# Recording the statistics of layer 1's norm at other places among the evacuations of a q and k set

## The chip, the cores and the metric

The kernel runs on one core of one Trainium2 chip. The metric is device time in microseconds (us) of a whole execution; lower is better. Engines: PE is TensorE (matmuls), PEld its weight load, DVE is VectorE, ACT is ScalarE, POOL is GpSimd, SP issues most DMAs.

## The reference

Two layers of masked attention over 64 graphs of 256 nodes with 512 features. Each normalises, applies Relu, attends within the graph and adds to x.

```python
h = jnp.maximum(_layernorm(x), 0.0)
x = x + _L0_gnn_ref(h, adj, Wq, Wk, Wv, Wo, bo)       # 4 heads of 64
h = jnp.maximum(_layernorm(x), 0.0)
x = x + _L1_gnn_ref(h, adj, gamma, beta, w_qkv, w_out, b_out)   # 8 heads of 64
```

`_L1_gnn_ref` begins with a second norm, of h itself:

```python
mu = jnp.mean(x, axis=-1, keepdims=True)
var = jnp.mean(jnp.square(x - mu), axis=-1, keepdims=True)
h = (x - mu) * jax.lax.rsqrt(var + LN_EPS) * gamma + beta
```

So layer 1 needs statistics twice for each row: those of x, and those of Relu(x - mean).

## The kernel before

A step is two graphs (512 rows: NT = 4 tiles of 128 rows, 512 features each), and there are NSTEP = 32 steps. The function `fast_path` doesn't loop over steps: it makes a list of events, each with a due time (period times 6.4 plus a place within the period), sorts it, and calls the functions in that order (L1251). The four compute engines run their instructions in the order in which these calls record them, so a place is a position in each engine's queue. Work of three steps is interleaved: while step s - 1 is in layer 1, layer 0 of step s is finished and its layer 1 norm begins, and layer 0 of step s + 1 is started.

**Projections.** A product of matrices is split Strassen-like into 7 products, numbered 1 to 7 and issued in the order SET = (1, 6, 5, 2, 7, 3, 4). `project_qk` (L791) issues 8 matmuls of 256 columns for each (L803), and returns a function that evacuates the bank. `at_set` spreads a set over one unit of places: product i is due at place + i/7, its evacuation at place + (i+1)/7 - 0.001 (`at_dense`, L1059). The set of this study is layer 1's second q and k set, recorded at AT_QK = 3.5 (L1209), so that its evacuations are due at 3.642 (product 1, on ACT, L737), 3.785 (6, DVE, L739), 3.928 (5, DVE, L741), 4.070 (2, ACT, L745), 4.213 (7, DVE, L743), 4.356 (3, DVE, L747) and 4.499 (4, DVE, L749).

**Banks.** Four banks serve all such products. Three are used twice: the second product is added onto the first in the bank, once that has been read out.

```python
SHARED = {2: 1, 4: 7, 3: 5}
```

**Layer 1's norm.** `norm1(s, k)` (L625) takes row tile NORM1[k] of the step's x: bn_stats and bn_aggr on DVE (`moments`, L574 to L577), then on ACT a negation of the mean (L633) and Relu(x - mean) into h (L634). x comes from layer 0's output (`combine` at AT_C0 = 3.0), whose last additions are POOL's (L771). `norm1_rest(s, k)` (L640) does `moments` of h, and with the fourth tile POOL makes row scales of all (L649, L650, and L586 to L588, `row_scales`). At 4.4998 ACT scales the rows (`scale_row`, L592), then DVE turns blocks of them (L686) and SP moves them.

**What else is recorded near.** At 4.499 ACT places the rows of the following step's layer 0 (`place_h`, L709), at 4.4995 POOL makes the sums of it that products need (`act_sums0`, `act_sums1`, L409 to L414); from 4.4997 the visit of the attention pair of heads: key sums on PE (L1007), reciprocals on DVE (L1029), weighted values (L976) and their copies on ACT (L988), scores (L920), masks on DVE (L944), exponentials on ACT (L949). From 4.5 PE runs layer 0's q and k set of the following step (L803 again), where POOL's sums are read from the second product on.

For the first and the last step (edge 0 and 1) there are other places; steps 1 to 30 (edge 2) take the third tuple of each row of the diff.

Of the kernel before, what the change touches and what calls it, by code (L numbers as in the profile page):

```python
# [315 lines left out]
def fast_path(  # L316
# [739 lines left out]
    def at(period, place, fn, *args):  # L1056
        events.append((period * (PERIOD if period >= 0 else FIRST) + place, len(events), fn, args))
# [52 lines left out]
    p = NSTEP - 2  # L1110
# [15 lines left out]
    for s in range(NSTEP):  # L1126

        p = s - 2
# [40 lines left out]
        p = s - 1  # L1169
        if s == 0:  # L1170
            p -= 2.23 / FIRST
        edge = 0 if s == 0 else 1 if s == NSTEP - 1 else 2
# [11 lines left out]
            else:  # L1184
                at_dense(p, AT_C0 + i / 14, 1 / 14, combine, s, 0, n)
        for k in range(NT):
            at(p, ((2.901, 3.041, 3.181, 3.321), (2.99919, 2.99933, 2.99947, 2.99961), (3.7, 3.72, 3.8, 3.82))[edge][k], norm1, s, k)
            at(
                p, ((3.042, 3.182, 3.322, 3.323), (2.99948, 3.2, 3.3, 3.45), (3.95, 4.02, 4.09, 4.2))[edge][k],
                norm1_rest, s, k,  # L1190
            )
            at(p, (10.9 + 0.1 * k, 6.5 + 0.1 * k, 5.6 + 0.01 * k)[edge], second_bias, s, k)
            place = ((3.6112, 3.6113, 3.7502, 3.7503)[k], 3.6 + 0.01 * k, AT_Q0 - 0.0002 + 0.00001 * k)[edge]
            at(p, place, scale_row, s, NORM1[k])
            if edge == 2:
                at(p, AT_Q0 + (0.15, 0.16, 0.29, 0.3)[k], turn_blocks, s, 1, NORM1[k])
# [8 lines left out]
        p = s  # L1205
        if s < NSTEP - 1:
# [3 lines left out]
            p, place = (s + 1, 1.0) if s < NSTEP - 2 else (s, LAST_QK + 2)  # L1210
# [4 lines left out]
        else:  # L1215
            p = s - 1
# [38 lines left out]
def kernel(tc, *args):  # L1255
    nc = tc.nc
    B, N, _ = args[0].shape
    P = 128
    with tc.tile_pool(name="guard", bufs=1) as guard:
        extremes = guard.tile([P, B // 2 * 6], FP, name="extremes")  # L1260
        ident = guard.tile([P, P], FP, name="ident")
        make_identity(nc, ident)
        fast_path(tc, *args, ident, extremes)
        safe = guard.tile([1, 1], I32, name="safe")
        with tc.tile_pool(name="gps", bufs=1, space=bass.MemoryType.PSUM) as ps:
            top = guard.tile([P, 1], FP, name="top")
            nc.vector.tensor_reduce(top, extremes, axis=mybir.AxisListType.X, op=ALU.max)
            row = ps.tile([1, P], FP, name="row")
            nc.tensor.transpose(row, top, ident)
            all_top = guard.tile([1, 1], FP, name="all_top")  # L1270
            nc.vector.tensor_reduce(all_top, row, axis=mybir.AxisListType.X, op=ALU.max)
            nc.vector.tensor_scalar(safe, all_top, LIMIT, None, op0=ALU.is_le)
        flag = nc.values_load(safe[0:1, 0:1], min_val=0, max_val=1, skip_runtime_bounds_check_because="a comparison gives 0 or 1")
        with tc.If(flag < 1):
            general_path(tc, *args)
# [29 lines left out]
```

## Time and profile before

| | |
|---|---|
| median of 3 runs | 3263.24 us (3262.0 to 3267.05) |
| profiled execution | 3261.14 us, its span 3259.3 us |
| TensorE clock granted | 0.999 |
| DMA | 237.04 MB, mean 73 GB/s |

The span is what the trace covers. In the lines of a timeline the first number is the start in us from the span's start, the second the duration in us (of all when several are merged), then engine, source line, operation, output and input tiles, and how many; a bracket gives the idle time before and what ended it. In a line of waits the numbers are total us, times, and the longest.

### The profile page before, as it was taken

How to read it: one execution, taken by the hardware profiler on the slowest of the kernel's cores; microseconds unless marked ns; L12 is line 12 of the kernel's file. 1: busy time of each engine (PE TensorE's matmuls, PEld its weight loads, DVE VectorE, ACT ScalarE, POOL GpSimd, SP SyncE). 2: the span in 40 equal slices, each digit the busy share in tenths (PEclk: the TensorE clock that was granted, in tenths of full speed). 3: DMA queues.
4: the chain of work that ended last, by engine and by line, in shares of the span. 5: the costliest groups of instructions: out<-in, count | busy, mean ns of one | idle time of the engine just before them, and what ended most of it. 6: DMA issues, size and time to landing. Idle time of an engine off the chain costs nothing.

```text
span 3259.3 us, 59763 instructions
## 1 busy us (share of the span) xinstructions
PE 3204.8 (98%) x22002; PEld 2611.8 (80%) x22002; DVE 2095.1 (64%) x3680; ACT 1256.6 (39%) x2226; POOL 2241.4 (69%) x2124
## 2 busy tenths in 40 slices
PE   9999999999999999999999999999999999999999
PEld 6787878888887888788787888888787888878777
DVE  6656666666666666676666666666666666666665
ACT  4434343343433334343434334343333434343431
POOL 7776776777766767667677677776776766767653
PEclk9999999999999999999999999999999999999999
DMA  4122232232322322223223222222232222322211
GB/s 147 43 85 77 55 85 65 79 82 53 85 69 73 88 60 71 76 67 86 76 55 85 62 82 81 53 84 66 75 86 62 72 70 73 86 72 57 85 31 47
DMA packets 214217, 237.04 MB, mean 73 GB/s; under 512 B 75032, under 2 KB 128416, under 8 KB 213920
## 3 DMA queue, kind: packets, MB, share of 16 engines
q1 hardware_dynamic: 213488, 232.76, 26.0%
q8 instruction: 177, 2.90, 0.4%
q14 instruction: 120, 0.98, 0.1%
q10 hardware_dynamic: 432, 0.40, 0.0%
HBM read 86.12 MB, written 33.62 MB: 37 GB/s over the span
## 4 chain that ended last, share of the span: by engine, by line
PE 66%; POOL 13%; DVE 11%; DMA 5%; SPq 4%; issue 1%; ACT 0%; POOLq 0%; DVEq 0%; ACTq 0%
PE mm L803 26%; PE mm L860 12%; PE sc L976 9%; PE mm L830 7%; PE sc L920 6%; DVE bs L576 5%; SPq L1041 4%; PE mm L1007 3%; POOL xt L498 3%; DMA xt<-in_x_dram 2%; POOL xt L771 2%; POOL n L563 2%; PE mm L920 2%; DVE p L944 2%; DMA oT<-oT 2%
## 5 line engine op out<-in xcount | busy, mean ns | idle before, releaser
L803 PE MATMUL mm<-hT,wqkv 128*128 128x256 f32 x3584 | 795.7, 381 | 31.7 <-DVE qk L743 31.7
L803 PEld LDWEIGHTS mm<-hT,wqkv 128*128 128x128 f32 x3584 | 675.7, 190 | 144.8 <-DVE qk L743 43.7
L953 POOL TENSOR_TENSOR pd<-p 128x512 f32<-128x512 f32 x383 | 479.7, 1274 | 328.1 <-ACT p L949 327.6
L860 PE MATMUL mm<-wo,oT 128*128 128x256 f32 x2632 | 588.3, 381 | 7.6 <-POOL oT L412 5.2
L860 PEld LDWEIGHTS mm<-wo,oT 128*128 128x128 f32 x2632 | 498.9, 191 | 87.1 <-issue 8.8
L1029 DVE RECIPROCAL oT<-mm 128x128 f32<-128x128 f32 x376 | 345.6, 940 | 249.6 <-PE mm L1007 245.6
L949 ACT ACTIVATE p<-p 128x512 f32<-128x512 f32 x766 | 439.6, 626 | 137.0 <-DVE p L944 137.0
L944 DVE TENSOR_TENSOR p<-sc,n 128x512 f32<-128x512 f32 x579 | 363.5, 684 | 113.9 <-PE sc L920 112.5
L844 PE MATMUL mm<-wqkv,hT 128*128 128x256 f32 x1792 | 401.9, 382 | 0.0
L803 PE MATMUL mm<-hT,wqk 128*128 128x256 f32 x1792 | 398.9, 382 | 0.3 <-ACT qk L737 0.2
L803 PEld LDWEIGHTS mm<-hT,wqk 128*128 128x128 f32 x1792 | 338.2, 191 | 56.3 <-issue 10.7
L844 PEld LDWEIGHTS mm<-wqkv,hT 128*128 128x128 f32 x1792 | 335.5, 190 | 53.8 <-issue 10.7
L976 PE MATMUL sc<-p,v 128*32 128x256 f32 x6128 | 350.0, 379 | 1.0 <-issue 1.0
L976 PEld LDWEIGHTS sc<-p,v 128*32 128x32 f32 x6128 | 199.7, 110 | 132.9 <-issue 1.8
L988 ACT COPY oT<-sc 128x512 f32<-128x512 f32 x188 | 109.4, 582 | 500.2 <-PE sc L976 495.3
L1046 POOL TENSOR_TENSOR oT<-oT 128x512 f32<-128x512 f32 x188 | 240.0, 1277 | 83.2 <-DMA oT<-oT 73.5
L920 PE MATMUL sc<-qk 64*128 64x256 f32 x2320 | 292.6, 385 | 0.0
L920 PEld LDWEIGHTS sc<-qk 64*128 64x128 f32 x2320 | 218.7, 186 | 58.8 <-issue 39.6
L771 POOL TENSOR_TENSOR xt<-xt,u 128x512 f32<-128x512 f32 x183 | 228.9, 1272 | 4.4 <-DVE xt L760 1.9
L830 PE MATMUL mm<-wv,hT 128*128 128x256 f32 x1024 | 227.0, 379 | 0.4 <-DVE qk L747 0.4
L830 PEld LDWEIGHTS mm<-wv,hT 128*128 128x128 f32 x1024 | 194.2, 190 | 27.3 <-DVE qk L747 0.7
L592 ACT ACTIVATE h<-h,mr,r 128x512 f32<-128x512 f32 x252 | 184.6, 804 | 0.0
(139 smaller groups left out, 3781.8 us busy)
## 6 DMA issues: line engine op xcount, KB each, us to landing
h<-blocks SPq DMA_DIRECT2D x960, 64.0 KB, 2.0
oT<-oT SPq DMA_DIRECT2D x1504, 32.0 KB, 1.9
xt<-in_x_dram SPq DMA_DIRECT2D x31, 1024.0 KB, 5.8
h<-in_x_dram SPq DMA_DIRECT2D x31, 1024.0 KB, 5.5
out_dram<-xt SPq DMA_DIRECT2D x31, 1024.0 KB, 4.5
ne<-row SPq DMA_DIRECT2D x30, 256.0 KB, 4.7
ad<-in_adj_dram SPq DMA_DIRECT2D x32, 128.0 KB, 8.7
wr<-in_L_gnn_w_qkv_dram SPq DMA_DIRECT2D x3, 1024.0 KB, 9.2
```

The lines of the kernel that those rows point to most:

```text
L771: (nc.vector if last else nc.gpsimd).tensor_tensor(r, r, u, ALU.add)
L803: nc.tensor.matmul(bank[:, k, :], w[:, wa, c, k, a * P:(a + 1) * P], st["hT"][:, ba, c, :], start=first and (k, c) == (0, 0), stop=(k, c) ...
L830: nc.tensor.matmul(bank, st["hT"][:, b0 + t // NIC * step, c % HC, i:i + P], wv0[:, c, :], start=(c == 0), stop=(c == NC - 1),)
L844: nc.tensor.matmul(bank[:, t, :], st["hT"][:, ba, c, t * P:(t + 1) * P], wqkv1[:, wa, c, 2, :], start=first and (t, c) == (0, 0), stop=(t, ...
L860: nc.tensor.matmul(bank[:, t, :], oT[:, ba, c, t * P:(t + 1) * P], w[:, wa, c, :], start=first and (t, c) == (0, 0), stop=(t, c) == (NIC - ...
L920: nc.tensor.matmul(sc[g][e][:, kc, :], qk[rows, 1, k0:k0 + P], qk[rows, 0, g * N:(g + 1) * N], start=True, stop=True,)
L944: nc.vector.tensor_tensor(p[e][:, g], sc[e], neg[:, :, g, :], ALU.add)
L949: nc.scalar.activation(p[e][:, g], p[e][:, g], AF.Exp, scale=SCALE)
L953: nc.gpsimd.tensor_tensor(pd[:, e], p[e][:, :, 0, :], p[e][:, :, 1, :], ALU.add)
L976: nc.tensor.matmul(po[r0:r0 + 32, g, :], st[f"v{lyr}"][:, g * NIC + kc, pr * P + r0:pr * P + r0 + 32], p[r0 // DH][:, g, kc, :], start=(kc ...
L1029: nc.vector.reciprocal(inv[:, k * P:(k + 1) * P], sums[:, k * P:(k + 1) * P])
L1046: nc.gpsimd.tensor_tensor(dst, dst, invb, ALU.mult)
```

## The change

Only two lines of the event list differ, and in them only the tuple for steps 1 to 30: the places of `norm1` and `norm1_rest`. No instruction is added or removed.

```diff
         for k in range(NT):
-            at(p, ((2.901, 3.041, 3.181, 3.321), (2.99919, 2.99933, 2.99947, 2.99961), (3.7, 3.72, 3.8, 3.82))[edge][k], norm1, s, k)
+            at(p, ((2.901, 3.041, 3.181, 3.321), (2.99919, 2.99933, 2.99947, 2.99961), (3.79, 3.8, 3.94, 3.95))[edge][k], norm1, s, k)
             at(
-                p, ((3.042, 3.182, 3.322, 3.323), (2.99948, 3.2, 3.3, 3.45), (3.95, 4.02, 4.09, 4.2))[edge][k],
+                p, ((3.042, 3.182, 3.322, 3.323), (2.99948, 3.2, 3.3, 3.45), (4.08, 4.22, 4.23, 4.37))[edge][k],
                 norm1_rest, s, k,
             )
```

Against the evacuations of the set, the order before is: evacuation 1; norm1 k0, k1; evacuation 6; norm1 k2, k3; evacuation 5; norm1_rest k0, k1; evacuation 2; norm1_rest k2, k3; evacuations 7, 3, 4. After: evacuations 1, 6; norm1 k0, k1; evacuation 5; norm1 k2, k3; evacuation 2; norm1_rest k0; evacuation 7; norm1_rest k1, k2; evacuation 3; norm1_rest k3; evacuation 4.

## The prediction

> **What bounds the kernel now.** I read the busy shares first, then the waits of the tensor engine (PE), then the timeline of one visit to the place that the diff names, on each engine. The times 1541 to 1603 us are one period of some 100 us; the 30 steady periods (layer 1's norm of steps 1 to 30) look alike.
>
> ```profile
> PE 3204.8 (98%) x22002; PEld 2611.8 (80%) x22002; DVE 2095.1 (64%) x3680; ACT 1256.6 (39%) x2226; POOL 2241.4 (69%) x2124
> ```
>
> PE is the bound; no other engine is above 69%. So time can be won only where PE pauses or takes longer than it must. The waits of PE (total us, times, longest) say where it pauses:
>
> ```profile
> PE mm L803 <- DVE qk L743: 31.7, 30, 1.8
> PE mm L720 <- ACT h L618: 6.9, 2, 6.7
> PE mm L860 <- POOL oT L412: 5.2, 1, 5.2
> ```
>
> Only the first comes every period, once in each. L803 is the matmul of a q and k set, L743 the evacuation of its product 7. Product 4 goes into the bank that product 7 has left (the table SHARED), so it can't start before VectorE (DVE) has read product 7 out. The PE timeline of the visit, and of the set that follows (layer 0's, as many matmuls of the same size), start and duration first:
>
> ```profile
> 1541.07 10.52 PE L803 MATMUL mm<-hT,wqkv 128*128 128x256 f32 x48
> 1552.45 1.99 PE L803 MATMUL mm<-hT,wqkv 128*128 128x256 f32 x8 [0.86 <-DVE qk L743]
> 1554.38 1.07 PE L1007 MATMUL mm<-pd,ones 128*32 128x256 f32 x16
> ...
> 1562.49 12.35 PE L803 MATMUL mm<-hT,wqk 128*128 128x256 f32 x56
> 1574.68 7.07 PE L830 MATMUL mm<-wv,hT 128*128 128x256 f32 x32
> ```
>
> From first matmul to the first of the next stage the undisturbed set takes 1574.68 - 1562.49 = 12.19 us, the stalled one 1554.38 - 1541.07 = 13.31. The loss is 1.12 us here, more than the 0.86 named, because a matmul's modelled end covers part of the gap. Read in the same way, the first q and k set of layer 1 takes 12.19 (1589.79 to 1601.98). Over the 30 visits the stalled set takes 13.01 to 14.54 us, mean 13.51. So the whole loss is (13.51 - 12.19) x 30 = 39.6 us, 1.2% of the time. Why the evacuation is late, DVE shows:
>
> ```profile
> 1545.76 0.67 DVE L739 TENSOR_TENSOR qk<-mm,qk 128x512 f32<-128x512 f32 x1
> ...
> 1547.96 0.66 DVE L741 TENSOR_TENSOR qk<-mm,qk 128x512 f32<-128x512 f32 x1
> 1548.54 0.69 DVE L576 BATCH_NORM_STATS2 bs<-h 128x6 f32<-128x512 f32 x1
> ...
> 1549.36 0.66 DVE L576 BATCH_NORM_STATS2 bs<-h 128x6 f32<-128x512 f32 x1
> ...
> 1550.15 0.66 DVE L576 BATCH_NORM_STATS2 bs<-h 128x6 f32<-128x512 f32 x1
> ...
> 1550.95 0.66 DVE L576 BATCH_NORM_STATS2 bs<-h 128x6 f32<-128x512 f32 x1
> ...
> 1551.74 0.66 DVE L743 TENSOR_TENSOR qk<-mm,qk 128x512 f32<-128x512 f32 x1
> 1552.32 0.68 DVE L747 TENSOR_TENSOR qk<-mm,qk 128x512 f32<-128x512 f32 x1
> ```
>
> Product 7's evacuation stands behind all four second statistics, recorded ahead of it. Before these, DVE had waited 2.18 us for GpSimd (POOL) to finish xt (L771), then done four first statistics. The queue never empties between.
>
> **What the Trainium skill says.** "Perfetto Trace Analysis", Identifying the Most-Contended Engine: busy matmul time is no good measure of the room left; the trace agrees (98% busy, 1.12 us lost where 0.86 is shown). The same page, Tensor Engine Instruction: ACT, DVE and GpSimd are strict FIFO; the DVE lines agree, L743 starting 0.79 us after the last bn_stats though its bank was ready long before. "PSUM — Partial Sum Buffer", PSUM bank collisions raise a hardware error: the hardware does not arbitrate two engines on one bank, so product 4's wait is needed and only an earlier evacuation shortens it; 30 waits in 30 periods agree. "SBUF — State Buffer", Who interferes with whom: a DVE instruction with one SBUF input, outside two-port modes, doesn't contend with GpSimd; bn_stats reads one, and L771 stays within 1256 to 1290 ns, so I charge nothing for new overlap.
>
> **The change, part by part.** I count t from the set's first matmul (1541.07). A product is 8 matmuls at 12.09/56 = 0.216 us (the chain gives the layer 0 stage of 56 matmuls at L860 as 12.09), so 1.73 us. Its evacuation can start 2.04 after its first matmul (1554.49 for L749, less 1552.45). Products 6, 5, 2, 7, 3, 4 are thus ready at t = 3.77, 5.49, 7.22, 8.94, 10.67, 12.4. A statistics pair (bn_stats, bn_aggr) holds DVE 0.82 after an evacuation, 0.79 after another pair (1548.54, 1549.36, 1550.15); an evacuation 0.58.
>
> - *First statistics (norm1).* k = 0, 1 move from 3.70, 3.72 to behind product 6's evacuation (due 3.785), k = 2, 3 from before to behind product 5's (3.928). Nothing is removed or added: 8 pairs, 6.4 us of DVE a period in both kernels. DVE now: evacuation 6 at 3.77, k0 4.36, k1 5.18, evacuation 5 at 5.97, k2 6.55, k3 7.37. xt is ready from POOL at 2.77 to 3.57 in 29 visits, 4.30 in the first: so k0 no longer waits for POOL.
> - *Second statistics (norm1_rest).* All four stood before evacuation 7 (due 4.213). Now k0 alone does (4.08), k1 and k2 follow it, k3 follows evacuation 3. So k0 8.16, evacuation 7 at 8.95, its data ready at 8.94. PE takes 0.71 from that start to product 4 (1551.74 to 1552.45): 9.66, and product 4 is due at 6 x 1.73 = 10.36. The wait vanishes with 0.70 us to spare. In the layer 1 set at 1589.79, evacuation 7 starts at 8.93 and no wait shows. Then k1 9.53, k2 10.35, evacuation 3 at 11.14, k3 11.72, evacuation 4 at 12.54, over by 13.2; the reciprocals (L1029) are due at 12.19 + 1.14 = 13.33. Gain: all of 39.6 us, if what follows is in time.
> - *ACT.* norm1 also issues a negation and a Relu (0.2 and 0.72 us) on ACT. k0's Relu ends at 6.5, k3's at 9.4, each ahead of its second statistics (8.16, 11.72). Product 2's evacuation, recorded behind k3's Relu, moves from 7.99 to about 9.5. Its bank and rows wait for the scores at 1558.83, t = 16.4 after the gain: hidden by 6 us.
> - *POOL.* The row scales (L649, L650, L586 to L588) end 2.87 us after the last bn_stats starts (1550.95 to 1553.82): 14.6 instead of 12.75. Behind them are the sums over layer 0's hT:
>
> ```profile
> 1553.62 0.20 POOL L588 TENSOR_TENSOR mr<-mr,r 128x4 f32<-128x4 f32 x1
> 1555.71 1.28 POOL L409 TENSOR_TENSOR hT<-hT 128x512 f32<-128x512 f32 x1 [1.90 <-ACT hT L709]
> 1557.08 1.28 POOL L412 TENSOR_TENSOR hT<-hT 128x512 f32<-128x512 f32 x1
> ```
>
> They could start at 14.64 - 1.32 = 13.3 and start at 14.7; L412's, wanted first, ends at 17.4, and PE reads it in the second product of layer 0's set at 12.19 + 8.11 + 1.73 = 22.0. Cover 4.6 us.
> - *Scaled rows.* ACT applies them (L592) behind the output copies, at 17.05 after the gain: 2.4 us after 14.6. The moved steps issue no DMA and pass nothing on SP.
>
> Sum: 3261.14 (profiled execution: span 3259.3 and 1.84 around it) - 39.6 = 3221.5. The median shown lies 2.10 higher, 3263.24: **3223.6**, given as 3223.5.
>
> **Rivals.**
> 1. *Part of the wait stays (about 3243).* Evacuation 7 has 0.70 us of slack behind seven DVE slots. A delay of 1.4 us in that queue would leave half the loss, 20 us. For: the POOL chain before xt varies by 0.8 us between visits. Against: xt is needed only at 4.36, and a late xt pushes fewer statistics in front of evacuation 7 (five pairs for eight), so it can't be later than before.
> 2. *The loss moves down (3263).* PE starts the next stage 1.3 us earlier and then waits for a chain that isn't PE's. For: POOL and DVE carry chains through DMA. Against: PE waits nowhere else every period, and these chains start from PE's own sums and scores, so they move up with it.
> 3. *Slower (about 3286).* ACT is one queue: if the row scales come after 17.05, L592 holds it, behind it the exponentials and the evacuation of layer 0's product 1. This ends at 1565.15 and PE needs its bank at 1562.49 + 3 x 1.73 = 1567.7. So PE loses time once the scales are 2.4 + 2.5 = 4.9 us later than counted, and more than was gained from 6.2; at 7 us it is 0.8 x 30 = 23 us slower. Only the move of k3 works towards this, and it makes 1.9.
> 4. *The order isn't what the numbers say.* Due times sort by value; all eight places fall between the evacuations named. I give it no chance of its own.
>
> **How the numbers follow.** Full gain 0.76 (3218 to 3229: between 42 and 34 us gained, with the spread of 3262 to 3267 in mind); rival 1 0.12; rival 2 0.06; rival 3 0.06. The measurement tells about 0.2%, 6.5 us, from no change: faster 0.88, same 0.06, slower 0.06. The range reaches into rival 1: 3217 to 3243.
>
> **What would show it.** Right: PE's wait on L743 at L803 gone or below 3 us in all; the set at 12.2 us to the key sums; DVE's wait on L771 gone; evacuation 7 near t = 9.0; POOL's wait for L709's hT gone. Wrong: a new periodic line in PE's waits (L803 on ACT L737, or on POOL L409 to L414), or L743 still there, behind k0.

## The result and the profile after

The changed kernel takes 3223.9 us (median, 3222.97 to 3224.88), against 3264.55 us for the kernel before measured beside it. The ratio is 0.9876, 95% interval 0.9858 to 0.9893: 1.2% faster, 40.7 us by the medians. The profiled execution took 3224.29 us, its span is 3222.4 us.

Busy shares of the kernel after, from the page. The span is 36.9 us shorter; PE's idle time fell by 28.7 of these (from 54.5 to 25.8), its busy time by 8.2. So about a fifth of what the stall cost had been shown as busy time.

```profile
PE 3196.6 (99%) x22002; PEld 2613.9 (81%) x22002; DVE 2091.9 (65%) x3680; ACT 1256.4 (39%) x2226; POOL 2240.0 (70%) x2124
```

The waits of PE in the kernel after (total us, times, longest). The wait of L803 on L743 fell from 31.7 us in 30 to 0.6 us in one, at 26.35 us in the program's first q and k set, which the change doesn't reach; none is left in the 30 visits, and no other line of this list comes once a period.

```profile
PE mm L720 <- ACT h L618: 7.6, 3, 6.6
PE mm L860 <- POOL oT L412: 5.8, 2, 5.5
PE mm L860 <- DVE xt L760: 3.1, 6, 0.7
PE mm L803 <- DVE qk L743: 0.6, 1, 0.6
```

PE's timeline of one visit of the kernel after (start, duration). The set is one run of 56 matmuls and the key sums follow 1536.25 - 1524.07 = 12.18 us after its start. Over the 30 visits the mean is 12.18, against 13.51 before; (13.51 - 12.18) x 30 = 39.9 us, close to the 40.7 us by the medians.

```profile
1524.07 12.25 PE L803 MATMUL mm<-hT,wqkv 128*128 128x256 f32 x56
1536.25 1.07 PE L1007 MATMUL mm<-pd,ones 128*32 128x256 f32 x16
```

DVE's timeline of the same visit. Evacuation 6 (L739) now comes when PE has made it ready, no longer behind the wait for POOL; one second statistic (bs<-h) stands ahead of evacuation 7 (L743), and this starts at t = 8.92, 1.75 us earlier than at 1551.74 before (t = 10.67).

```profile
1527.79 0.69 DVE L739 TENSOR_TENSOR qk<-mm,qk 128x512 f32<-128x512 f32 x1 [2.83 <-PE mm L803]
...
1530.01 0.66 DVE L741 TENSOR_TENSOR qk<-mm,qk 128x512 f32<-128x512 f32 x1
...
1532.20 0.66 DVE L576 BATCH_NORM_STATS2 bs<-h 128x6 f32<-128x512 f32 x1
...
1532.99 0.66 DVE L743 TENSOR_TENSOR qk<-mm,qk 128x512 f32<-128x512 f32 x1
1533.57 0.68 DVE L576 BATCH_NORM_STATS2 bs<-h 128x6 f32<-128x512 f32 x1
...
1536.57 0.66 DVE L749 TENSOR_TENSOR qk<-mm,qk 128x512 f32<-128x512 f32 x1
1537.39 1.77 DVE L1029 RECIPROCAL oT<-mm 128x128 f32<-128x128 f32 x2 [0.16 <-PE mm L1007]
```

POOL in the same visit: the row scales (L588 is their last) now end where the sums over layer 0's hT could already have begun; the 1.90 us wait in front of L409 is gone.

```profile
1538.44 0.20 POOL L588 TENSOR_TENSOR mr<-mr,r 128x4 f32<-128x4 f32 x1
1538.60 1.28 POOL L409 TENSOR_TENSOR hT<-hT 128x512 f32<-128x512 f32 x1
1539.96 1.27 POOL L412 TENSOR_TENSOR hT<-hT 128x512 f32<-128x512 f32 x1
```

### The profile page after: what moved, and what is told of

It reads as the page before. It is cut to its first block, busy times and chain, and to the rows that moved or that the text cites. A ratio compares the mean times of both kernels' runs of the same rounds, so it can differ in the third digit from the quotient of the medians.

```text
span 3222.4 us, 59733 instructions
## 1 busy us (share of the span) xinstructions
PE 3196.6 (99%) x22002; PEld 2613.9 (81%) x22002; DVE 2091.9 (65%) x3680; ACT 1256.4 (39%) x2226; POOL 2240.0 (70%) x2124
## 4 chain that ended last, share of the span: by engine, by line
PE 93%; DMA 2%; POOL 2%; SPq 1%; issue 1%; DVE 1%; POOLq 0%; DVEq 0%
PE mm L803 36%; PE mm L860 17%; PE mm L844 10%; PE sc L976 10%; PE sc L920 8%; PE mm L830 7%; PE mm L1007 3%; PE mm L920 2%; SPq L1041 1%; DMA xt<-in_x_dram 1%; POOL xt L498 1%; PE mm L886 0%; DMA h<-in_x_dram 0%; DVE oT L1029 0%; PE mm L549 0%
## 5 line engine op out<-in xcount | busy, mean ns | idle before, releaser
L803 PE MATMUL mm<-hT,wqkv 128*128 128x256 f32 x3584 | 787.5, 380 | 0.0
L803 PEld LDWEIGHTS mm<-hT,wqkv 128*128 128x128 f32 x3584 | 678.2, 190 | 102.4 <-issue 11.4
L860 PE MATMUL mm<-wo,oT 128*128 128x256 f32 x2632 | 587.9, 381 | 9.1 <-POOL oT L412 5.8
L860 PEld LDWEIGHTS mm<-wo,oT 128*128 128x128 f32 x2632 | 498.2, 190 | 89.0 <-issue 7.7
L803 PE MATMUL mm<-hT,wqk 128*128 128x256 f32 x1792 | 398.9, 382 | 0.8 <-DVE qk L743 0.6
L803 PEld LDWEIGHTS mm<-hT,wqk 128*128 128x128 f32 x1792 | 338.2, 191 | 56.8 <-issue 11.2
L920 PEld LDWEIGHTS sc<-qk 64*128 64x128 f32 x2320 | 218.9, 186 | 58.9 <-issue 39.6
L592 ACT ACTIVATE h<-h,mr,r 128x512 f32<-128x512 f32 x252 | 184.6, 804 | 0.0
```

What stands on the lines that cost most here:

```text
L803: nc.tensor.matmul(bank[:, k, :], w[:, wa, c, k, a * P:(a + 1) * P], st["hT"][:, ba, c, :], start=first and (k, c) == (0, 0), stop=(k, c) ...
L860: nc.tensor.matmul(bank[:, t, :], oT[:, ba, c, t * P:(t + 1) * P], w[:, wa, c, :], start=first and (t, c) == (0, 0), stop=(t, c) == (NIC - ...
L920: nc.tensor.matmul(sc[g][e][:, kc, :], qk[rows, 1, k0:k0 + P], qk[rows, 0, g * N:(g + 1) * N], start=True, stop=True,)
```

## Experiments: which part of the change makes the gain

The theory: the gain is what lies between product 5's and product 7's evacuation in DVE's queue. Rivals: it is the filling of DVE's 2.2 us wait for POOL, or the spreading as such, or the amount of DVE's work in the set. Each run is stated as a difference from the changed kernel or from the kernel before, and none leaves out work of the reference. As in the prediction, t counts from the set's first matmul. Diffs of norm1_rest's places show only the end of the line, the tuple for steps 1 to 30.

**First half only.** From the changed kernel:

```diff
-(4.08, 4.22, 4.23, 4.37))[edge][k],   # norm1_rest
+(3.96, 4.02, 4.09, 4.2))[edge][k],
```

> The changed kernel with only its first half: norm1 at its new places, norm1_rest back at the old ones (3.96 for k0, so that it stays behind norm1 k3). Ahead of evacuation 7 stand four second statistics, behind norm1 k2 and k3. Theory (what counts is how many statistics stand between product 5's and product 7's evacuation on VectorE): evacuation 7 starts at t = 5.94 + 0.58 + 6 x 0.80 = 11.3, the set takes 14.0 us, 1.8 more than in the changed kernel, so 3224 + 54 = 3278 us, slower than the kernel before. Rival (the gain is the filling of VectorE's 2.2 us wait for GpSimd ahead of the first statistics): VectorE no longer waits, so 3224 to 3235.

3275.6 us, ratio to the kernel before 1.0043 (1.0029 to 1.0057): slower than it. Its PE waits:

```profile
PE mm L803 <- DVE qk L743: 46.1, 31, 1.7
```

DVE's timeline of a visit at 2960.2: evacuation 6 is as early as in the changed kernel and DVE doesn't wait for POOL, yet evacuation 7 starts at t = 11.31, behind six statistics (two first ones, k2 and k3, and all four second ones).

```profile
2963.92 0.69 DVE L739 TENSOR_TENSOR qk<-mm,qk 128x512 f32<-128x512 f32 x1 [2.83 <-PE mm L803]
...
2966.14 0.66 DVE L741 TENSOR_TENSOR qk<-mm,qk 128x512 f32<-128x512 f32 x1
...
2970.71 0.66 DVE L576 BATCH_NORM_STATS2 bs<-h 128x6 f32<-128x512 f32 x1
...
2971.51 0.66 DVE L743 TENSOR_TENSOR qk<-mm,qk 128x512 f32<-128x512 f32 x1
```

So filling DVE's wait is worth nothing here, and that rival falls.

**Second half only.** The kernel before with the new places of norm1_rest:

```diff
-(3.95, 4.02, 4.09, 4.2))[edge][k],
+(4.08, 4.22, 4.23, 4.37))[edge][k],
```

> The kernel before with only the second half of the change: norm1 at its old places, norm1_rest at the new ones. Theory: VectorE still waits for GpSimd ahead of the first statistics, but only one second statistic stands ahead of evacuation 7, at t = 2.8 to 3.6 + 4.6, so at most 8.2, before its bank is ready at 8.94: the whole gain, 3224 us. Rival (filling the wait): nothing is filled, 3260 us or more.

3222.3 us, 0.9882 (0.9866 to 0.9897): the whole gain, with norm1 untouched. The set takes 12.18 us.

**Two moves only.** The kernel before, k2 and k3 of norm1_rest put right behind evacuation 7:

```diff
-(3.95, 4.02, 4.09, 4.2))[edge][k],
+(3.95, 4.02, 4.22, 4.23))[edge][k],
```

> The kernel before with only norm1_rest k2 and k3 moved, to just behind evacuation 7 (4.22, 4.23). Theory: evacuation 7 starts 6.0 us after the first statistic, which GpSimd lets start at t = 2.8 to 3.6, so at 8.9 to 9.6, within the 9.65: the whole gain from two moves, 3224 to 3226 us. Rival (the first statistics have to move too, or the second ones have to be spread): 3240 or more.

3223.3 us, 0.9882 (0.9866 to 0.9897). The set takes 12.22 in the mean. Neither spreading nor the first half is needed: two of eight moves carry everything.

**Two, and three, second statistics ahead of evacuation 7.** From the changed kernel, in turn:

```diff
-(4.08, 4.22, 4.23, 4.37))[edge][k],
+(4.08, 4.09, 4.23, 4.37))[edge][k],   # two ahead
+(4.08, 4.09, 4.1, 4.37))[edge][k],    # three ahead
```

> The changed kernel with two second statistics ahead of evacuation 7 instead of one (k1 at 4.09). Theory: evacuation 7 at t = 9.73, 0.8 later, just past the 9.65 at which PE begins to wait: 0.1 to 0.2 us a visit, 3226 to 3230 us. Rival (any delay of this evacuation costs its full length): 0.8 x 30 = 24 us, 3248.

> The changed kernel with three second statistics ahead of evacuation 7 (k1 at 4.09, k2 at 4.1). Theory: evacuation 7 at t = 10.53, the set takes 2.64 from there as in the kernel before, so 13.2, 1.0 more than undisturbed: 3224 + 30 = 3254 us. Rival (filling the wait): 3224 to 3230.

3227.1 us (0.9896, 0.9881 to 0.9911) and 3251.3 us (0.9968, 0.9956 to 0.9981). With the first run they make a series:

| second statistics ahead | evacuation 7 starts at t | set, us | added to 12.18, x 30 | time, us |
|---|---|---|---|---|
| 1 (second half only) | 8.83 | 12.18 | 0 | 3222.3 |
| 2 | 9.73 | 12.37 | 5.7 | 3227.1 |
| 3 | 10.51 | 13.15 | 29.1 | 3251.3 |
| 4 (first half only) | 11.31 | 13.95 | 53.1 | 3275.6 |

The fourth column added to the first time gives 3228.0, 3251.4 and 3275.4, within 0.9 us of what was measured. The second statistic ahead costs a fifth to a quarter of its length, each further one its full 0.8 us; a price of 0.8 us for every place, the rival of the run with two ahead, falls. The limit is the prediction's 9.65: in the traces with two, three and four ahead, product 4 starts 0.71 us after evacuation 7, as in the kernel before, and it is due at 10.36. On top comes a small fixed price: where PE had to wait, in every visit of these kernels, the key sums follow the start of product 4 by 1.92 us, in the unbroken set by 1.82. So a visit costs the delay beyond 9.65 plus 0.10, which is 0.18 for two ahead (9.73). PE's timeline of a visit with two ahead shows why such small waits need the start-to-start times: the list of waits names none for them, and the run of 56 matmuls isn't broken, but the next stage comes 12.36 us after it begins.

```profile
2913.51 12.43 PE L803 MATMUL mm<-hT,wqkv 128*128 128x256 f32 x56
2925.87 1.07 PE L1007 MATMUL mm<-pd,ones 128*32 128x256 f32 x16
```

**More statistics behind evacuation 7.** From the changed kernel, k1's second moments taken three times (the same numbers):

```diff
-        moments(mg, h, t)
+        for _ in range(3 if k == 1 and 0 < s < NSTEP - 1 else 1):
+            moments(mg, h, t)
```

> The changed kernel with two pairs more of second statistics on VectorE (k1's moments three times, the result is the same), behind evacuation 7. Theory: VectorE's amount of work is not the bound and evacuations 3 and 4 have 1.2 us and more before anyone is late: 3224 to 3228 us for 1.6 us more of VectorE a visit. Rival (VectorE's work in the set is what counts, wherever it stands): 1.6 x 30 = 48, 3272 us.

3221.8 us, 0.9875 (0.986 to 0.9891): 1.6 us more DVE work a visit (DVE's busy time in all is 2130.0 us against 2091.9) cost nothing. Its last evacuation starts at t = 14.1 instead of 12.5 and the reciprocals at 14.67 instead of 13.32, but the masks of the scores at 17.86 against 17.80: ahead of these DVE had waited 1.20 us for PE's scores, and this wait is now used up. Much more work behind evacuation 7 would delay the masks; that wasn't run. Two pairs moved ahead of evacuation 7 (three ahead), also 1.6 us, cost 29 us. What counts here is the place, not the amount.

## Experiments: the covers that the prediction named

**GpSimd's sums, five and three copies more.** From the changed kernel, the first sum over layer 0's hT repeated behind itself (the same numbers):

```diff
         at(p, AT_Q0 - 0.0005 if s > 1 else FIRST_C0 + 0.1, lambda s=s: act_sums0(S[s]["hT"]))
+        for _ in range(5 if s > 1 else 0):     # 3 in the other run
+            at(p, AT_Q0 - 0.0005, lambda s=s: act_sums0(S[s]["hT"]))
```

> The changed kernel with five more copies of the first of GpSimd's sums over layer 0's hT, put behind the first (the result is the same), so that the second sum, which PE's second product of layer 0's set reads, ends 6.2 us later. It tests the cover of 4.6 us that the prediction gave for row scales that end later. Theory: PE wants that sum at t = 22.0, it comes at 17.2 + 6.2 = 23.4: 1.4 to 1.6 us a visit, so 3266 to 3272 us, with a new wait of L803 for L412. Rival (GpSimd is not on the path at all, 70% busy): 3224. Rival (no cover, each us on GpSimd is a us of time): 3224 + 186 = 3410.

> The changed kernel with three more copies of GpSimd's first sum, where e5 had five. In e5 a copy took 1.36 us, so the second sum comes 4.1 us later, at t = 21.2, and PE wants it at 22.0. Theory (a cover of 4.8 us, as the traces of the changed kernel and of e5 give): no loss, 3222 to 3225 us. Rival (GpSimd's delay is felt in proportion, 58 us for 6.8 a visit): 3/5 of it, 3258.

Five: 3281.7 us, 1.006 (1.0046 to 1.0073). Three: 3223.3 us, 0.9878 (0.9863 to 0.9893). With five, the timelines of POOL and of PE in a visit that began at 2765.13:

```profile
2779.67 8.06 POOL L409 TENSOR_TENSOR hT<-hT 128x512 f32<-128x512 f32 x6
2787.80 1.27 POOL L412 TENSOR_TENSOR hT<-hT 128x512 f32<-128x512 f32 x1
```

```profile
2785.42 1.99 PE L803 MATMUL mm<-hT,wqk 128*128 128x256 f32 x8
2789.13 10.63 PE L803 MATMUL mm<-hT,wqk 128*128 128x256 f32 x48 [1.72 <-POOL hT L412]
```

The second sum ends at 2789.07 (t = 23.94), and PE's second product, due at 2785.42 + 1.73 (t = 22.02), starts at 24.00: 1.98 us late, x 30 = 59, and 3281.7 is 58 above the run with three copies. The threshold was right; my expectation of 1.4 to 1.6 us took a copy at 1.23 us, the spacing of the later sums, while copies of one sum, each rewriting the tile just written, follow each other at (8.06 - 1.28)/5 = 1.36. In the changed kernel the second sum ends at 1541.23, t = 17.16: the cover that row scales ending later eat into is 4.9 us, 4.6 by the prediction. It holds for 4.1 us more and not for 6.8.

**Row scales behind the sums.** From the changed kernel, the row scales taken out of `norm1_rest` and recorded after `act_sums1`:

```diff
-            ve = stat.tile([P, part], FP, name="ve1", bufs=2)
-            ...
-            row_scales(s, ve, rows, k < 2 or part == NT)
+            def scales():
+                ...
+            st["scales"] = scales        # at once for the first and last step
...
         if edge == 2:
             at(p, AT_Q0 + 0.31, move_blocks, s)
+            at(p, AT_Q0 - 0.00035, lambda s=s: S[s].pop("scales")())
```

> The changed kernel with GpSimd's row scales recorded behind the sums over layer 0's hT instead of ahead of them. It tests the rival by which late row scales hold ACT's queue. Theory: the sums run a us earlier, the row scales end at t = 20.6 instead of 14.6, ACT waits 3.5 us in front of L592, with the exponentials behind it; PE's slack behind that (the bank of layer 0's product 1) is another 2.5 us, so the wait is hidden: 3224 us. Rival: the exponentials' delay reaches PE at once: 3224 + 3.5 x 30 = 3329.

3248.9 us, 0.996 (0.9946 to 0.9973): 25 us slower than the changed kernel, neither of the expected times. The order that the change left alone, row scales ahead of sums, is worth those 25 us. ACT's timeline of the visit at 1535.41 (lines of this kernel are 5 higher from `norm1_rest` on), and PE's:

```profile
1556.28 2.93 ACT L592 ACTIVATE h<-h,mr,r 128x512 f32<-128x512 f32 x4 [3.51 <-POOL mr L588]
1559.11 2.17 ACT L954 ACTIVATE p<-p 128x512 f32<-128x512 f32 x4
1561.19 0.56 ACT L742 COPY qk<-mm 128x512 f32<-128x512 f32 x1
```

```profile
1561.80 3.50 PE L808 MATMUL mm<-hT,wqk 128*128 128x256 f32 x15 [0.66 <-ACT qk L742]
```

ACT stands 3.51 us before it scales the rows; the evacuation of layer 0's product 1 (L742), queued behind the exponentials, ends at 1561.75, and PE's product 2 starts at t = 26.39 instead of 20.29 + 3 x 1.73 = 25.48: 0.91 x 30 = 27 us. My expectation had the right pieces and a wrong end: a delay of 3.5 us isn't hidden by 2.5 us of slack, 1.0 is left over. So the prediction's third rival is a real mechanism, at about two thirds of the price named there (by its rule PE loses once the scales come 4.9 us later than 14.6; here they come 6.2 later and it loses 0.91, not 1.3). The change, which made them 1.8 later, stays clear of it.

## Experiment: the same wait one stage earlier

DVE's timeline of the stage just ahead of the set, layer 0's combine, in the changed kernel: product 4's evacuation (L765) comes 1.12 us after product 3's (L767), where the others follow each other at 0.79 to 0.88. Product 4 shares a bank with product 7 (the second L760) and only product 3's four matmuls lie between; the list of waits shows nearly nothing of it.

```profile
1522.29 0.69 DVE L760 TENSOR_TENSOR xt<-mm,xt 128x512 f32<-128x512 f32 x1
1523.15 0.69 DVE L767 TENSOR_TENSOR xt<-mm,xt 128x512 f32<-128x512 f32 x1 [0.17 <-PE mm L860]
1524.27 0.69 DVE L765 TENSOR_TENSOR xt<-mm,xt 128x512 f32<-128x512 f32 x1 [0.42 <-PE mm L860]
```

```diff
-    SETC0 = (1, 6, 5, 2, 7, 3, 4)
+    SETC0 = (1, 5, 6, 7, 2, 3, 4)
```

> The changed kernel with layer 0's combine products in the order 1, 5, 6, 7, 2, 3, 4 instead of 1, 6, 5, 2, 7, 3, 4, so that two products of four matmuls, not one, lie between product 7 and product 4, which shares its bank. Theory (the same kind of wait, too short to be named: the stage takes 6.29 us for 28 matmuls that need 6.04, and product 4's evacuation comes 1.12 us after product 3's, not 0.86): 0.25 x 30 = 7 us less, 3215 to 3218. Rival (the 0.25 us lies in starting the stage): 3223, or more if the first statistics, whose rows are finished on GpSimd in another rhythm, come late.

3211.9 us, 0.9846 (0.9833 to 0.986): faster than both kernels, by 11.4 us against the run with three copies, which was measured beside it. The stage's 28 matmuls, from the first to the start of the next stage, in PE's timeline of this kernel:

```profile
2005.18 6.21 PE L860 MATMUL mm<-wo,oT 128*128 128x256 f32 x28
2011.22 12.25 PE L803 MATMUL mm<-hT,wqkv 128*128 128x256 f32 x56
```

That is 6.04 us, and so it is in all 29 visits after the first. In the changed kernel most take 6.29 or 6.30 (1524.07 - 1517.77): there the seven products start 0.86 us apart, but product 4 starts 1.04 after product 3 and the next stage 0.94 after product 4. In the new order all are 0.86. So the loss lay where the theory put it, 0.25 x 30 = 7.5 us.

The gain is larger because seven visits of the changed kernel were worse, 6.48 to 7.45 us: product 7's evacuation came later still (the line L860 <- L760 in the waits of the kernel after), and these waits went too. Over the 29 visits the traces differ by 10.9 us from the changed kernel and by 9.1 from the run with three copies; the other 2.3 us against that run lie in the first 150 us. PE's wait of the first period for GpSimd's sums over oT, 5.8 us in all in the changed kernel and 2.6 here, brings less than that: the set behind it is 2.1 us longer in the same visit.

## Why the prediction was right, point by point

- **Bound and loss.** Predicted 39.6 us from the stretch of the stalled set against an undisturbed one; the set's mean fell from 13.51 to 12.18 (12.19 was forecast), 39.9 us. The list of waits gave 31.7 for it, and would have been a fifth short. Why a visit loses 1.12 where 0.86 is named, the prediction explains in part: product 4 starts at 11.39 instead of 10.36, 1.03 late, so a modelled end can hide 0.17; the remaining 0.10 is the slower restart found above. (The stage of 56 matmuls at L860 from which it took 12.09 is layer 1's, not layer 0's, which has 28; the price of a matmul is the same.) Predicted 3223.5, measured 3223.9.
- **First statistics.** Predicted k0 at 4.36 and evacuation 5 at 5.97, found at 4.33 and 5.94. k0 no longer waits for POOL, except in the first visit (5.04), whose set takes 12.28. The prediction didn't say that this half carries none of the gain; alone it costs 14 us against the kernel before.
- **Second statistics.** Predicted evacuation 7 at 8.95, 3 at 11.14, 4 at 12.54; found 8.92, 11.11, 12.50. The limit of 9.65 stands by the series, and in the first visit, where evacuation 7 starts at 9.65, product 4 starts on time at 10.36 and the set takes 12.28, longer by just that 0.10. The prediction had 0.70 us to spare, and 0.73 is there, less than one statistic. That "only an earlier evacuation" shortens product 4's wait was too narrow: another order of the products did it in the combine. And the 30 waits show that the program makes PE wait for the bank; what the hardware does without that no run here shows.
- **ACT.** Product 2's evacuation predicted at about 9.5, found at 9.22 (1533.29); nobody waits for it.
- **POOL and the scaled rows.** Row scales predicted to end at 14.6, found at 14.57; covers of 4.6 and 2.4 us predicted, 4.9 and 2.7 found. L592 starts at 17.25, not 17.05: the prediction took the mean gain of 1.32 off a visit (18.38) that lost only 1.12. The experiments passed the first at 4.1 and broke it at 6.8, and showed the second, with the 2.5 us of slack behind it, broken at 6.2.
- **Rivals.** Nothing stayed of the wait in the 30 visits, and no chain below took it up. "PE waits nowhere else every period", said against the second rival, was wrong by the 0.25 us a visit in the combine, a wait that no change of these places touches. The places do what their numbers say: the order on DVE is the one listed.
- **From profile to median.** The two profiled executions differ by 36.9 us, the medians by 40.7. The spans add up: the 30 sets give 39.9 us, 1.3 are lost ahead of the first changed visit (it begins at 134.39 and at 135.65), which the change can't reach, and 1.6 in the irregular waits of the other 29 combines. For a profiled execution the prediction's sum was 3221.5, and 3224.29 was measured, while the kernel before came out at 3264.55 beside it, not 3263.24. That the median was met to 0.4 us is thus luck in part: the runs of one kernel spread by 2 to 5 us. The mechanism and the 39.6 us were not luck.

## What to carry to other kernels

When one engine both frees the banks of a saturated TensorE and does other work, find the one evacuation for which a matmul waits, note the time by which it must start, and count what stands ahead of it in that queue: up to that time work was free in these runs, and beyond it each piece cost its length. Measure such a loss from stage start to stage start against an undisturbed twin of the stage in the same trace, since idle time (28.7 us here of the 36.9 won) and named waits (31.7 of the 39.9) show too little of it. And look at all short stages with a reused bank: the wait may be there without a line that names it, and another order of the products can remove it.

## What was not expected of the hardware

- PE's waits of 0.18 us (two statistics ahead) and 0.25 us (combine) a visit left no regular line among its waits, though they cost about 5 and 7.5 us in all.
- After a wait for its bank PE lost 0.10 us more than the wait: 1.92 us instead of 1.82 from the start of product 4 to the key sums, in the kernel before and in the runs with two, three and four ahead.
- GpSimd sums of the same size follow each other at 1.36 us where the second rewrites the tile just written (the copies of L409) or reads it (L412, 1539.96 after L409's 1538.60), and at 1.23 where it does neither (L413 at 1541.19).
